# Small VectorE operations written as scalar-tensor-tensor with a constant column, in a four-layer graph attention kernel

## The chip, the core and the metric

The kernel runs on one core of a Trainium2 chip, as one launch. The metric is the device time of that core in microseconds (us). The kernel was run three times: 1598.85, 1600.91 and 1601.07 us, median 1600.91. One more execution was taken with the hardware profiler; it has a time of its own, 1596.83 us, and all durations below come from it.

The core's engines run side by side, each through its own list of instructions, and meet at semaphores: TensorE (PE, with its weight loads shown as PEld), VectorE (DVE), ScalarE (ACT), GpSimd (POOL) and SyncE (SP, which here only issues DMAs). The ordinary loads and stores are issued by SyncE, the indirect gathers by GpSimd.

## The reference

Four graph layers are applied one after the other to `x` (8 graphs, 2048 nodes, 64 features). All share one 2048 x 2048 adjacency matrix, which is sparse. Each layer is residual, with a normalisation ahead of it:

```python
h = jnp.maximum(_layernorm(x), 0.0);  x = x + _L0_gnn_ref(h, adj)
h = jnp.maximum(_layernorm(x), 0.0);  x = x + _L1_gnn_ref(h, adj, W1, a1)
h = jnp.maximum(_layernorm(x), 0.0);  x = x + _L2_gnn_ref(h, adj, Wh, bh, Wo, bo, gamma, beta)
h = jnp.maximum(_layernorm(x), 0.0);  x = x + _L3_gnn_ref(h, adj, W3, a3)
```

`_L0` is dot-product attention of a node over its neighbours: masked scores `h_n . h_m / 8`, softmax, weighted sum of `h_m`. `_L1` and `_L3` are additive attention: the score of an edge is `leaky_relu(f1_n + f2_m)`, where `f1` and `f2` are two projections of `h W`; what follows is elu or relu. `_L2` runs dot-product attention with four heads (the node itself counts as its neighbour), a leaky relu and an output projection, then a second dot-product attention on the result, then a layer norm with gamma and beta. A neighbour that is missing gets a large negative score, so it has no weight in the softmax.

## The kernel before

The kernel does not form the 2048 x 2048 scores. It turns the adjacency into lists of neighbours and works edge by edge. Nodes stand in 16 row tiles of 128 (`NT`), one node in each partition, with the features of all 8 graphs side by side (`F` = 512 columns, `B` = 8 graphs of `D` = 64). Nodes with low numbers have more neighbours, and a row tile `i` needs `ROWS[i]` slots (`K`) in which every node has one neighbour, and `PACKED[i]` slots (`T`) in which the further edges of the tile are packed 128 to a slot. `ROWS` holds 1 twice and 2 five times, `PACKED` holds 1 eight times; the total is 81 slots.

The work is done in five passes that read tables in HBM:

- First stage, up to about 350 us: `load_adj` and `lists` build the lists of a row tile from its rows of the adjacency, while the first attention layer runs on the tiles whose lists are ready. `lists` (L625 to L718) finds the neighbours with repeated maxima of eight on VectorE (L640, L652), lifts them off a constant (L645), turns them into gather indices (L662 for the row slots, L717 for the packed ones) and masks (L664, L680, L718), and makes the selection matrices that spread queries over packed edges (L689, L711). These arrays are narrow: L662 writes `K` numbers per partition, L664 writes `K - 1`, L717 and L718 write `T`. The sequence of L645, L654, L652, L657, L662 is a chain within VectorE. `lists` hands `idx` to the gathers, `mba` and `mbb` to the exponentials.
- Two additive layers (`additive(1, ...)` from about 350 to 600 us, and `additive(4, ...)` from about 1440 us to the end), whose scores are made at L540 to L549.
- The four-headed attention, about 600 to 1160 us (`score`, `weights`, `second2`).
- Its second attention, about 1160 to 1440 us (`first3` to `fourth3`), with L894 subtracting a row constant from the scores, and two normalisations for each tile.

A normalisation is `norm_a` (L257 to L276): sums of a row on VectorE (L261), then the mean (L265) and the centred rows (L268), either on GpSimd or on VectorE, as its caller asks; or, without centring, only the negative mean (L273). Its squares go to ScalarE, the rest is `norm_b`.

Neighbour rows are fetched by indirect DMAs that GpSimd issues (`gather`, L244), one for each slot, into a ring of 26 slots in SBUF. GpSimd also multiplies gathered rows with their weights in the first, third and fourth pass (`weigh_sum` L381 with GpSimd, `weights` L794 and L807), adds the residual (L480) and centres rows in the first stage. VectorE computes the products and sums of the scores (L423 to L432, L777, L781).

The order of the instructions on each engine is set by a scheduler: it takes the program as it is written tile by tile in `pipeline` (with lags between the stages of a tile) and orders each engine's list by an estimate of every instruction's duration. A changed instruction can therefore move its neighbours.

Behind the edge version stands a dense version (`gnn_stack`), which runs only if a check (`flag`) finds that the lists do not hold the adjacency. It isn't executed here.

Of the kernel before, what the change touches and what calls it, by code (L numbers as in the profile page):

```python
# [8 lines left out]
F32 = mybir.dt.float32  # L9
# [4 lines left out]
OP = mybir.AluOpType  # L14
AX = mybir.AxisListType

P = 128
NEG = -1.0e30
# [14 lines left out]
LIFT = 4096.0  # L33
# [32 lines left out]
def edge_stack(ctx: ExitStack, tc: tile.TileContext, x_in, adj, w1, w1t, a1, wh, wht, bh, wo, bo,  # L66
# [9 lines left out]
    nc = tc.nc  # L76
    N, F = x_in.shape
    D = gamma.shape[0]
    B = F // D
    NT = N // P  # L80
    H = bh.shape[0] // D
    INV_D = 1.0 / D
# [5 lines left out]
    const = ctx.enter_context(tc.tile_pool(name="const", bufs=1))  # L88
# [4 lines left out]
    nc.scalar.preload_act_table_set("natural_log_exp_and_others")  # L93
    eps = const.tile([P, 1], F32, name="eps")
    nc.gpsimd.memset(eps, EPS)
    ones = const.tile([P, 1], F32, name="ones")
    nc.gpsimd.memset(ones, 1.0 / N)

    idx = const.tile([P, NS], I32, name="idx")
    mba = const.tile([P, NS], F32, name="mba")  # L100
# [31 lines left out]
    def slots(t, i):  # L132
        return t[:, OFF[i]:OFF[i] + SLOTS[i]]
# [62 lines left out]
    def heads(t, n=B):  # L196
        return t.rearrange("p (b d) -> p b d", b=n)

    def wide(t, n=B):
        return t[:, :, None].to_broadcast([P, n, D])  # L200
# [22 lines left out]
    def rows(i, lo, hi, most=RING):  # L223

        t = lo
        while t < hi:
            at = (held[i] + t) % RING
            m = min(most, hi - t, RING - at)
            yield t, m, ring[:, at:at + m, :]
            t += m  # L230
# [24 lines left out]
    def rows_of(k, i):  # L255
        return table[k][i * P:(i + 1) * P, :F]

    def norm_a(src, st, centre, eng=nc.vector):

        s = small.tile([P, B], F32, name="ln_s")  # L260
        nc.vector.tensor_reduce(s, heads(src), AX.X, OP.add)  # L261
        st["sq"] = rows_pool[0].tile([P, F], F32, name="ln_sq", bufs=4)
        if centre:
            mean = small.tile([P, B], F32, name="ln_m")
            eng.tensor_scalar(mean, s, INV_D, None, op0=OP.mult)  # L265
            st["less"] = None
            st["src"] = rows_pool[0].tile([P, F], F32, name="ln_xc", bufs=3)
            eng.tensor_tensor(heads(st["src"]), heads(src), wide(mean), op=OP.subtract)  # L268
            nc.scalar.activation(st["sq"], st["src"], AF.Square)
            return  # L270
        st["src"] = src
        st["less"] = small.tile([P, B], F32, name="ln_m")
        nc.vector.tensor_scalar(st["less"], s, -INV_D, None, op0=OP.mult)  # L273
        for b in range(B):
            nc.scalar.activation(st["sq"][:, b * D:(b + 1) * D], src[:, b * D:(b + 1) * D], AF.Square,
                                 bias=st["less"][:, b:b + 1])  # L276
# [171 lines left out]
    def leaky(dst, src):  # L448
        return nc.vector.scalar_tensor_tensor(dst, src, SLOPE, src, op0=OP.mult, op1=OP.max)
# [21 lines left out]
    def divide(st, dst):  # L471
        nc.vector.tensor_tensor(heads(dst), heads(st["y"]), wide(st["rec"]), op=OP.mult)
# [40 lines left out]
    def additive(k, wd, *finish):  # L513
        def take(i, st):
            n = order.index(i)
            gather(k, i, st, taken[k, order[n - SPREAD]] if n >= SPREAD else None)

        def sums(i, st):
            w = slots(w_all, i)
            for t, m, g in rows(i, 0, SLOTS[i]):  # L520
                nc.scalar.activation(w[:, t:t + m], g[:, :, F:], AF.Exp, scale=1.0 / TEMP)
            d, p = by_query(i, w, B)
            S = seen[:, i, :]
            nc.vector.tensor_tensor(S, p, d, op=OP.add)

            z = small.tile([P, B], F32, name="z")
            nc.vector.tensor_scalar(z, S.bitcast(I32), TEMP * LN2 / 2 ** 23, -127.0 * TEMP * LN2, op0=OP.mult,
                                    op1=OP.add)
            nc.vector.tensor_tensor(z, z, f1s[:, i, 0, :], op=OP.add)
            leaky(f1s[:, i, 1, :], z)  # L530

        def first(i, st):
            K, T = ROWS[i], PACKED[i]
            w = slots(w_all, i)
            s = slots(s_all, i)
            n = 2 * B if k == 4 else B
            fs = f1s[:, i].rearrange("p t b -> p (t b)")[:, :n]
            pv = by_edge(i, fs, n)
            for t, m, g in rows(i, 0, K):
                nc.vector.tensor_tensor(s[:, t:t + m, :], g[:, :, F:], fs[:, None, :B].to_broadcast([P, m, B]),  # L540
                                        op=OP.add)
            for t, m, g in rows(i, K, K + T):
                nc.vector.tensor_tensor(s[:, t:t + m, :], g[:, :, F:], pv[:, t - K:t - K + m, :B], op=OP.add)
            taken[k, i] = leaky(s, s)
            if k == 4:
                nc.vector.tensor_tensor(s[:, :K, :], s[:, :K, :], fs[:, None, B:].to_broadcast([P, K, B]),
                                        op=OP.subtract)
                nc.vector.tensor_tensor(s[:, K:, :], s[:, K:, :], pv[:, :, B:], op=OP.subtract)
                nc.vector.tensor_scalar(s, s, 60.0, None, op0=OP.min)  # L549
            nc.scalar.activation(w, s, AF.Exp)  # L550
            wp = ps_w[0].tile([P, F], F32, name="w")[:, :(K + T) * B].rearrange("p (t b) -> p t b", b=B)
            nc.scalar.activation(wp, s, AF.Exp)
            st["wp"] = wp

        def check(i, st):
            second(i, st, st["wp"], seen[:, i, :] if k == 1 else None)

        def third(i, st):
            st["att"] = rows_pool[0].tile([P, F], F32, name="att")
            divide(st, st["att"])  # L560
            st["xt"] = transposed(st["att"])

        def project(i, st):
            p = st["p"] = ps_q.tile([P, F], F32, name="q")
            for j in range(F // P):
                nc.tensor.matmul(p[:, j * P:(j + 1) * P], st["xt"][:, j, :], wd, start=True, stop=True)
            finish[0](i, st)

        mid = [sums] if k == 4 else []
        pipeline(take, *mid, first, both(check, xs_rows), third, project, *finish[1:])  # L570

    def elu_add(i, st):
# [8 lines left out]
    with tc.tile_pool(name="rows", bufs=2) as rp:  # L581
        rows_pool[0] = rp
        sel_all[0] = rp.tile([P, sum(PACKED) * P], F32, name="sel", bufs=1)
        with tc.tile_pool(name="lists", bufs=2) as pool, \
# [39 lines left out]
            def lists(i, st):  # L624

                K, T, W = ROWS[i], PACKED[i], WIDTH[i]
# [15 lines left out]
                                nc.vector.match_replace(out=key[:, lo:hi], in_to_replace=c1[:, s, r, :],  # L642
                                                        in_values=key[:, lo:hi], imm_value=0.0)
                ends = c1.rearrange("p s r k -> p (s r k)")
                nc.vector.tensor_scalar(ends, ends, LIFT, 0.0, op0=OP.subtract, op1=OP.max)  # L645
                full = [s for s, (lo, hi) in enumerate(segs) if hi - lo > 8 * rounds]
                nc.vector.tensor_reduce(over[:, i, 0:1], c1[:, full[0]:, rounds - 1, 7:8].rearrange("p s o -> p (s o)"),
                                        AX.X, OP.max)
                ell = small.tile([P, W + 2], F32, name=f"ell{W}", bufs=2)
# [9 lines left out]
                at = OFF[i]  # L659
                me = nn[:, i:i + 1]  # L660
                nc.scalar.copy(ell[:, W + 1:W + 2], me)
                nc.vector.tensor_scalar(idx[:, at:at + K], ell[:, :K], -1.0, N + 1.0, op0=OP.mult, op1=OP.add)  # L662
                if K > 1:
                    nc.vector.tensor_scalar(mba[:, at + 1:at + K], ell[:, 1:K], 0.0, NEG, op0=OP.is_equal, op1=OP.mult)  # L664
                st8 = small.tile([P, 8], F32, name="st8")
                deg, half, nmid = st8[:, 0:1], st8[:, 1:2], st8[:, 2:3]
                junk = small.tile([P, W], F32, name=f"junk{W}", bufs=1)
# [9 lines left out]
                m = pm[:, P:P + K]  # L677
# [19 lines left out]
                ke = small.tile([P, max(PACKED)], F32, name="ke")[:, :T]  # L697
                V = W - K
                step = min(T, F // (V + 2))
                mp = mbb[:, at + K:at + K + T]  # L700
                for t0 in range(0, T, step):
# [7 lines left out]
                    for t in range(n):  # L709
                        eq = pool.tile([P, P], F32, name="eq")  # L710
                        nc.vector.scalar_tensor_tensor(eq[:, :V], iotaj[:, :V], col[:, t:t + 1], pv[:, t, :V],  # L711
                                                       op0=OP.is_equal, op1=OP.mult,
                                                       accum_out=ke[:, t0 + t:t0 + t + 1])
                    nc.vector.tensor_scalar(qidx[:, POFF[i] + t0:POFF[i] + t0 + n], pv[:, :, V + 1], -1.0, N + 1.0,
                                            op0=OP.mult, op1=OP.add)
                    nc.vector.tensor_tensor(mp[:, t0:t0 + n], ke[:, t0:t0 + n], pv[:, :, V + 1], op=OP.is_equal)
                nc.vector.tensor_scalar(idx[:, at + K:at + K + T], ke, -1.0, N + 1.0, op0=OP.mult, op1=OP.add)  # L717
                nc.vector.tensor_scalar(mp, mp, NEG, None, op0=OP.mult)  # L718

            pipeline(xin_rows, lambda i, st: norm_a(st["x"], st, True, nc.gpsimd), pre_b,  # L720
                     pre_c(None, nc.vector), pre_d(0, None))
# [152 lines left out]
    with tc.tile_pool(name="ps_q", bufs=3, space=bass.MemoryType.PSUM) as ps_q, \  # L874
# [11 lines left out]
        def first3(i, st):  # L886
            K = ROWS[i]
            sq = rows_pool[0].tile([P, F], F32, name="sq")
            nc.scalar.activation(sq, st["rows"], AF.Square)
            c = small.tile([P, B], F32, name="c3")  # L890
            nc.vector.tensor_reduce(c, heads(sq), AX.X, OP.add)
            s, w = scores(i, st, st["rows"]), slots(w_all, i)
            pv = by_edge(i, c, B)
            nc.vector.tensor_tensor(s[:, :K], s[:, :K], c[:, None, :].to_broadcast([P, K, B]), op=OP.subtract)  # L894
            nc.vector.tensor_tensor(s[:, K:], s[:, K:], pv, op=OP.subtract)
            exps(i, w, s, mbb, 1.0)

# [44 lines left out]
        v = small.tile([P, 4], F32, name="v", bufs=1)  # L942
# [520 lines left out]
```

## Time and profile before

| | |
|---|---|
| median of three runs | 1600.91 us |
| the profiled execution | 1596.83 us |
| its span, first to last instruction | 1595.0 us |
| mean granted TensorE clock | 0.899 |
| busy: PE, DVE, POOL, ACT | 1295.0, 1242.0, 1006.4, 768.0 us |
| gathers at L244 (405), GpSimd | 389.3 us, 961 ns each |
| GpSimd products L381, L794 | 156.6 us at 1736 ns; 307.2 us at 1918 ns |
| VectorE rows of the first stage, 120 to 270 us | 138.9 us busy of 150 |

"Busy" is the time in which an engine had an instruction running, and that includes the time in which a running instruction stands still inside the engine. A small VectorE instruction whose duration is far above that of its like is such a case: there is no idle time ahead of it that a semaphore explains, the time lies within it. This is why the mean of a group can hide two kinds of rows, and why groups are best read with different shapes kept apart.

A line of the groups holds: source line, engine, operation, output and inputs, their shapes, the count, then busy us and mean ns of one, then idle time before. A line of the timeline holds the start, the length, the engine, the source line and the operation.

### The profile page before, as it was taken

What the parts mean: (1) busy time and instruction counts of PE and PEld (TensorE: products, weight loads), DVE (VectorE), ACT (ScalarE), POOL (GpSimd) and SP (SyncE); (2) the same over time, 40 slices, a digit from 0 to 9 for tenths busy, and PEclk for the clock granted to TensorE, in tenths of its full rate; (3) what the DMA queues carried; (4) which work ended last, traced back from release to release, by engine and by line L of the source; (5) the groups of instructions that cost most, each with busy time, mean ns of one, the idle gap of its engine ahead of it and who ended that gap; (6) DMA issues with size and microseconds to landing.
All of it is one profiled execution on the core that took longest, in us unless ns stands there. A gap on an engine that the chain in (4) does not pass through costs nothing.

```text
span 1595.0 us, 16633 instructions
## 1 busy us (share of the span) xinstructions
PE 1295.0 (81%) x4280; PEld 671.0 (42%) x4280; DVE 1242.0 (78%) x2489; ACT 768.0 (48%) x2475; POOL 1006.4 (63%) x844
## 2 busy tenths in 40 slices
PE   3768898995989771899987999999747788975888
PEld 1624354564544430344343444443323354563555
DVE  5998989854689776999998799871159999974666
ACT  3424555672557781465541455555424446680111
POOL 6336777766750007998789889898278486306650
PEclk9997887987999996899999999999968798957899
DMA  7775654536874449465266345400085354136761
GB/s 216 233 244 158 201 183 152 198 107 182 260 253 153 173 164 348 161 232 173 88 209 204 111 141 182 158 14 7 27 321 154 93 179 126 67 103 204 244 205 69
DMA packets 88177, 266.99 MB, mean 167 GB/s; under 512 B 14957, under 2 KB 15001, under 8 KB 79881
## 3 DMA queue, kind: packets, MB, share of 16 engines
q0 software_dynamic: 37392, 141.05, 28.3%
q1 hardware_dynamic: 50680, 124.80, 22.6%
q8 instruction: 36, 0.59, 0.2%
q14 instruction: 69, 0.56, 0.1%
HBM read 208.74 MB, written 57.05 MB: 167 GB/s over the span
## 4 chain that ended last, share of the span: by engine, by line
PE 24%; DVE 13%; POOL 8%; DMA 7%; ACT 6%; issue 5%; SPq 0%; POOLq 0%; DVEq 0%; ACTq 0%
PE y L809 10%; DMA g<-table,idx 4%; POOL wh L794 3%; POOL g L244 3%; DMA rows<-table 3%; PE y L386 3%; PE y L801 2%; PE m L846 2%; ACT yn L817 2%; PE m L858 2%; DVE s L781 2%; DVE prod L777 2%; DVE prod L423 1%; POOL wh L807 1%; PE m L842 1%
## 5 line engine op out<-in xcount | busy, mean ns | idle before, releaser
L244 POOL DMA_INDIRECT g<-table,idx x405 | 389.3, 961 | 268.3 <-issue 115.6
L794 POOL TENSOR_TENSOR wh<-g,w 128x1024 f32<-128x1024 f32 x162 | 307.2, 1918 | 35.8 <-PE y L809 33.9
L386 PE MATMUL y<-wg,ident 128*128 128x512 f32 x392 | 223.0, 696 | 22.6 <-POOL wg L381 12.7
L381 POOL TENSOR_TENSOR wg<-g,w 128x1024 f32<-128x1024 f32 (+1 forms) x91 | 156.6, 1736 | 75.2 <-ACT w L437 65.9
L781 DVE TENSOR_REDUCE s<-prod 128x32 f32<-128x2048 f32 x81 | 183.9, 2286 | 20.2 <-ACT w L783 19.8
L809 PE MATMUL y<-wh,ident 128*128 128x512 f32 x320 | 155.6, 614 | 23.7 <-POOL wh L807 21.5
L386 PE MATMUL y<-wg,selt 128*128 128x512 f32 x256 | 135.1, 634 | 4.6 <-POOL wg L381 2.9
L809 PE MATMUL y<-wh,selt 128*128 128x512 f32 x256 | 123.1, 605 | 13.2 <-POOL wh L794 13.2
L817 ACT ACTIVATE yn<-y,rec 128x64 f32<-128x64 f32 x512 | 111.3, 367 | 29.7 <-PE y L809 29.0
L386 PEld LDWEIGHTS y<-wg,ident 128*128 128x128 f32 x392 | 79.0, 219 | 106.6 <-issue 66.2
L777 DVE TENSOR_TENSOR prod<-q,g 128x2048 f32<-128x2048 f32 x49 | 111.5, 2275 | 3.7 <-ACT g L775 3.3
L381 DVE TENSOR_TENSOR wg<-g,w 128x1024 f32<-128x1024 f32 (+1 forms) x92 | 98.9, 1086 | 11.3 <-PE y L386 9.5
L443 DVE SCALAR_TENSOR_TENSOR zt<-m,bhc,att 128x512 f32<-128x512 f32 x64 | 47.1, 737 | 75.3 <-ACT att L442 75.3
L809 PEld LDWEIGHTS y<-wh,ident 128*128 128x128 f32 x320 | 59.4, 195 | 98.6 <-issue 62.4
L400 PE MATMUL m<-w,selt 128*128 128x8 f32 (+1 forms) x384 | 58.8, 255 | 50.7 <-ACT w L437 16.5
L400 PEld LDWEIGHTS m<-w,selt 128*128 128x128 f32 x384 | 60.8, 205 | 92.9 <-ACT w L437 26.8
L775 ACT COPY g<-g 128x512 f32<-128x512 f32 x81 | 50.4, 622 | 84.5 <-DVE prod L777 83.6
L429 PE MATMUL q<-rows,sel 128*128 128x512 f32 x128 | 79.8, 725 | 12.7 <-DVE prod L431 4.7
L801 PE MATMUL y<-rows,ident 128*128 128x512 f32 x128 | 70.9, 640 | 19.6 <-DMA rows<-table 14.4
L777 DVE TENSOR_TENSOR prod<-qe,g 128x2048 f32<-128x2048 f32 x32 | 73.0, 2281 | 13.9 <-DMA qe<-qtab,qidx 12.7
L357 PE MATMUL m<-ones,xh 128*128 128x1 f32 x384 | 70.6, 307 | 10.7 <-DVE idx L717 3.5
L357 PEld LDWEIGHTS m<-ones,xh 128*128 128x128 f32 x384 | 70.8, 274 | 20.0 <-issue 13.2
(221 smaller groups left out, 2673.0 us busy)
## 6 DMA issues: line engine op xcount, KB each, us to landing
qtab<-q SPq DMA_DIRECT2D x16, 1040.0 KB, 4.1
a<-in_adj_dram SPq DMA_DIRECT2D x32, 512.0 KB, 5.1
q<-qtab SPq DMA_DIRECT2D x14, 1040.0 KB, 5.3
table<-xh SPq DMA_DIRECT2D x48, 256.0 KB, 3.3
rows<-table SPq DMA_DIRECT2D x48, 256.0 KB, 4.1
xs<-x SPq DMA_DIRECT2D x48, 256.0 KB, 2.2
x<-xs SPq DMA_DIRECT2D x48, 256.0 KB, 3.3
table<-xh SPq DMA_DIRECT2D x32, 260.0 KB, 2.1
```

The costliest lines, as they stand in the source:

```text
L244: g = nc.gpsimd.indirect_dma_start(out=ring[:, (held[i] + t) % RING, :cols], out_offset=None, in_=table[k][:, :], in_offset=bass.IndirectO ...
L357: nc.tensor.matmul(p[:, c:c + 1], xh[:, c * P:(c + 1) * P], ones, start=True, stop=True)
L381: eng.tensor_tensor(wg[:, :m].rearrange("p t (b d) -> p t b d", b=B), g[:, :, :F].rearrange("p t (b d) -> p t b d", b=B), w[:, t0:t0 + m, ...
L386: nc.tensor.matmul(y, lhs(i, t), wg[:, t - t0, :], start=(t == 0 and own is None), stop=(t == n - 1))
L400: nc.tensor.matmul(p[:, :cols], selt(i, t), packed[:, t, :], start=(t == 0), stop=(t == T - 1))
L429: nc.tensor.matmul(qe, sel(i, t - K), q, start=True, stop=True)
L777: nc.vector.tensor_tensor(pr.rearrange("p (b h) d -> p b h d", h=H), q[:, :B * H * D].rearrange("p (b h d) -> p b h d", h=H, d=D), heads(g ...
L781: nc.vector.tensor_reduce(s[:, t - lo, :], pr, AX.X, OP.add)
L794: nc.gpsimd.tensor_tensor(wg, heads(row(i, t))[:, :, None, :].to_broadcast([P, B, 2, D]), w[:, :, 2 * k:2 * k + 2, None].to_broadcast([P, ...
L801: nc.tensor.matmul(st["ys"][j], ident, xb[:, 4 * j:4 * j + 4], start=True, stop=False)
L809: nc.tensor.matmul(st["ys"][j], lhs(i, t), wg[:, 4 * j:4 * j + 4], start=False, stop=(t == n - 1))
L817: nc.scalar.activation(yn[:, b, h, :], st["ys"][j][:, b, h, :], AF.Copy, scale=st["rec"][:, 4 * j + b, 2 * k + h:2 * k + h + 1])
```

## The change

Three constant columns of 128 x 1 are made at the start: `zero` (0.0), `np1` (N + 1) and `neg1` (holds `NEG`). Small VectorE operations on SBUF data are then written as `scalar_tensor_tensor`, which computes `(in0 op0 scalar) op1 in1`, with one of these columns, repeated along the row, as `in1`. Where the operation already had two tensors, it keeps them and gets a factor of 1.0. Operations that GpSimd does, and those with an operand in PSUM, stay as they are. The numbers computed are the same.

```diff
+    zero, np1, neg1 = (const.tile([P, 1], F32, name=name) for name in ("zero", "np1", "neg1"))
+    for t, v in ((zero, 0.0), (np1, N + 1.0), (neg1, NEG)):
+        nc.gpsimd.memset(t, v)
...
+    def alike(t, like):
+        return t.to_broadcast(like.shape)
+
+    def times(dst, src, k):
+        nc.vector.scalar_tensor_tensor(dst, src, k, alike(zero, src), op0=OP.mult, op1=OP.add)
+
+    def less_from(dst, src):
+        nc.vector.scalar_tensor_tensor(dst, src, -1.0, alike(np1, src), op0=OP.mult, op1=OP.add)
...
-            eng.tensor_scalar(mean, s, INV_D, None, op0=OP.mult)
+            if eng is nc.vector:
+                times(mean, s, INV_D)
+            else:
+                eng.tensor_scalar(mean, s, INV_D, None, op0=OP.mult)
...
-            eng.tensor_tensor(heads(st["src"]), heads(src), wide(mean), op=OP.subtract)
+            if eng is nc.vector:
+                nc.vector.scalar_tensor_tensor(heads(st["src"]), heads(src), 1.0, wide(mean), op0=OP.mult,
+                                               op1=OP.subtract)
+            else:
+                eng.tensor_tensor(heads(st["src"]), heads(src), wide(mean), op=OP.subtract)
...
-        nc.vector.tensor_scalar(st["less"], s, -INV_D, None, op0=OP.mult)
+        times(st["less"], s, -INV_D)
...
-                nc.vector.tensor_tensor(s[:, t:t + m, :], g[:, :, F:], fs[:, None, :B].to_broadcast([P, m, B]),
-                                        op=OP.add)
+                nc.vector.scalar_tensor_tensor(s[:, t:t + m, :], g[:, :, F:], 1.0,
+                                               fs[:, None, :B].to_broadcast([P, m, B]), op0=OP.mult, op1=OP.add)
...
-                nc.vector.tensor_scalar(ends, ends, LIFT, 0.0, op0=OP.subtract, op1=OP.max)
+                nc.vector.scalar_tensor_tensor(ends, ends, LIFT, alike(zero, ends), op0=OP.subtract, op1=OP.max)
...
-                nc.vector.tensor_scalar(idx[:, at:at + K], ell[:, :K], -1.0, N + 1.0, op0=OP.mult, op1=OP.add)
+                less_from(idx[:, at:at + K], ell[:, :K])
                 if K > 1:
-                    nc.vector.tensor_scalar(mba[:, at + 1:at + K], ell[:, 1:K], 0.0, NEG, op0=OP.is_equal, op1=OP.mult)
+                    nc.vector.scalar_tensor_tensor(mba[:, at + 1:at + K], ell[:, 1:K], 0.0, alike(neg1, ell[:, 1:K]),
+                                                   op0=OP.is_equal, op1=OP.mult)
...
-                nc.vector.tensor_scalar(idx[:, at + K:at + K + T], ke, -1.0, N + 1.0, op0=OP.mult, op1=OP.add)
-                nc.vector.tensor_scalar(mp, mp, NEG, None, op0=OP.mult)
+                less_from(idx[:, at + K:at + K + T], ke)
+                times(mp, mp, NEG)
...
-            nc.vector.tensor_tensor(s[:, :K], s[:, :K], c[:, None, :].to_broadcast([P, K, B]), op=OP.subtract)
+            nc.vector.scalar_tensor_tensor(s[:, :K], s[:, :K], 1.0, c[:, None, :].to_broadcast([P, K, B]),
+                                           op0=OP.mult, op1=OP.subtract)
```

The subtraction at L546 (the fifth pass) is rewritten in the same way as L540. In the order of the list above these are the lines L265, L268, L273, L540, L645, L662, L664, L717, L718 and L894 of the kernel before.

More of the change, by code (lines that the diff above doesn't have):

```diff
@@ L545, in first @@
             if k == 4:
-                nc.vector.tensor_tensor(s[:, :K, :], s[:, :K, :], fs[:, None, B:].to_broadcast([P, K, B]),
-                                        op=OP.subtract)
+                nc.vector.scalar_tensor_tensor(s[:, :K, :], s[:, :K, :], 1.0,
+                                               fs[:, None, B:].to_broadcast([P, K, B]), op0=OP.mult,
+                                               op1=OP.subtract)
                 nc.vector.tensor_tensor(s[:, K:, :], s[:, K:, :], pv[:, :, B:], op=OP.subtract)
```

## The prediction

> **What bounds the kernel now.** I read the table of stretches first, to see which engine is full in the stages where the rewritten instructions stand. The columns are time, then busy microseconds and instruction count of PE, PEld, DVE, ACT and POOL, the granted clock, the DMA share and GB/s.
>
> ```profile
> 70.00:120.00 50.00, 31.22 (x84) 13.08 (x83) 47.24 (x259) 14.12 (x26) 17.16 (x18) 1.00 0.66 215
> 120.00:170.00 50.00, 37.85 (x111) 19.03 (x111) 44.79 (x187) 23.97 (x71) 32.77 (x31) 0.75 0.60 186
> 170.00:220.00 50.00, 45.35 (x148) 20.88 (x148) 49.83 (x148) 26.36 (x85) 42.27 (x36) 0.94 0.58 188
> 220.00:270.00 50.00, 43.45 (x159) 24.75 (x159) 44.24 (x142) 25.73 (x100) 39.56 (x35) 0.77 0.48 148
> 270.00:320.00 50.00, 46.84 (x182) 29.30 (x182) 40.41 (x104) 32.21 (x129) 37.24 (x34) 0.86 0.55 190
> 360.00:600.00 240.00, 193.65 (x682) 103.91 (x682) 179.68 (x318) 150.73 (x446) 83.55 (x101) 0.92 0.60 200
> 1160.00:1440.00 280.00, 215.45 (x707) 120.70 (x707) 241.53 (x460) 152.61 (x529) 156.10 (x124) 0.79 0.44 144
> ```
>
> VectorE is the fullest engine of the first stage: 138.9 of the 150 us from 120 to 270, and 47.2 of the 50 before that. In the fourth pass (1160 to 1440) it has 241.5 of 280. The chain of waits reaches back only to about 590 us, so for the first stage the table has to serve. Next, the groups of instructions kept apart by shape (busy us, mean ns of one | idle before):
>
> ```profile
> L645 DVE TENSOR_SCALAR c<-c 128x64 f32<-128x64 f32 x14 | 8.4, 602 | 0.0
> L664 DVE TENSOR_SCALAR mba<-ell 128x2 f32<-128x2 f32 x6 | 7.4, 1236 | 0.0
> L664 DVE TENSOR_SCALAR mba<-ell 128x3 f32<-128x3 f32 x1 | 3.7, 3745 | 0.0
> L664 DVE TENSOR_SCALAR mba<-ell 128x1 f32<-128x1 f32 x5 | 0.7, 141 | 0.0
> L718 DVE TENSOR_SCALAR mbb<-mbb 128x3 f32<-128x3 f32 x2 | 3.3, 1635 | 0.0
> L718 DVE TENSOR_SCALAR mbb<-mbb 128x1 f32<-128x1 f32 x8 | 1.1, 142 | 0.0
> L894 DVE TENSOR_TENSOR s<-s,c 128x24 f32<-128x24 f32 x6 | 3.6, 602 | 0.0
> ```
>
> Two or three numbers per partition cannot take 1.2 to 3.7 us of arithmetic, while one number takes 0.14. The timeline shows what the long ones do (start us, us):
>
> ```profile
> 177.15 3.76 POOL L381 TENSOR_TENSOR wg<-g,w 128x1024 f32<-128x1024 f32 x2
> 178.14 2.81 DVE L664 TENSOR_SCALAR mba<-ell 128x2 f32<-128x2 f32 x1
> ...
> 193.47 1.92 POOL L381 TENSOR_TENSOR wg<-g,w 128x1024 f32<-128x1024 f32 x1
> 193.48 0.14 DVE L664 TENSOR_SCALAR mba<-ell 128x1 f32<-128x1 f32 x1
> ...
> 42.85 1.04 POOL L268 TENSOR_TENSOR ln_xc<-x,ln_m 128x512 f32<-128x512 f32 x1
> 43.45 0.99 DVE L313 SCALAR_TENSOR_TENSOR xh<-ln_xc,ln_r 128x512 f32<-128x512 f32 x1
> ...
> 1274.85 3.77 POOL L381 TENSOR_TENSOR wg<-g,w 128x1024 f32<-128x1024 f32 x2
> 1276.06 2.61 DVE L894 TENSOR_TENSOR s<-s,c 128x24 f32<-128x24 f32 x1
> ```
>
> At 178.14 a two-element tensor_scalar stands until both GpSimd products are over (180.91). At 193.48 a one-element one runs straight through a GpSimd product. The third pair matters most: a scalar_tensor_tensor with both inputs in SBUF, 0.68 us at its other places, takes 0.99 because GpSimd's subtraction runs until 43.89. The fourth is a tensor_tensor of two SBUF inputs that waits through two products. So three kinds of VectorE instruction wait for GpSimd: tensor_scalar of more than one element, tensor_tensor from SBUF and SBUF, and scalar_tensor_tensor from SBUF and SBUF.
>
> [...]
>
> **The change part by part.**
>
> 1. *tensor_scalar of two or more elements becomes scalar_tensor_tensor with a constant column* (L645 all 16; L662 14; L664 9; L717 8; L718 8; the 48 means at L265 and L273). [...] By the third pair it still waits for GpSimd. [...] no trace row here has a second input that never moves, so this is bounded from both sides. Upper end 0. Lower end, all waits gone: 14 x (0.602-0.18) = 5.9 at L645; 6.5 + 3.6 at L664; 2.1 + 0.4 at L662; 1.3 + 0.7 at L717; 3.0 + 0.4 at L718; together 24 us of VectorE in the first stage. I take 0, since L313's second input is itself one value repeated 64 times.
>
> 2. *tensor_scalar of one element becomes two-input.* By the shapes there are 23: 2 at L662, 5 at L664, 8 at L717, 8 at L718. They have no wait today (0.134 to 0.145 us) and get one. Two ways to size it. (a) The 55 longer rows of those five lines lose 24 us, 0.43 each; 23 x 0.43 = 10 us. (b) Laid on today's timeline, the one-element rows that start under a GpSimd tensor instruction, or in the last 0.4 us of a gather's descriptor work, stand at 193.48 (1.9 us to go), 252.12 and 253.27 (0.5 and 0.4), and 294.99 (4.7 us of GpSimd instructions end to end; the L718 behind it waits in the same gap): 7.5 us. Not all is on the path: after 294.99 VectorE has about 3.2 us of idle gaps (0.5 + 0.3 + 0.8 + 1.7) that take up part of the 4.7. So 1.9 + 0.9 + 1.5 = 4.3 us. What queues behind is the list building itself: L652's next maximum, then the indices that the gathers of this row tile need. Bounds: 0, if everything is absorbed, and 10.
>
> 3. [...] 14 rows of 128x64 go from about 0.18 to 0.204 (L449 at that size): 0.35 us. The 128x352 row goes from 0.329 to about 0.35 + 0.15 = 0.50, and the 128x128 row gains under 0.1. Sum 0.6 us, on VectorE in the full stage.
>
> 4. *tensor_tensor becomes scalar_tensor_tensor with a factor 1* (L540, L546, L894, and VectorE's L268). Two SBUF inputs before and after: 160 to 200 ns for the short ones, 680 for 512 elements either way (L313). The waits at L268 and L894 in the fourth pass (2.2 and 4.0 us in all) and at L265 (1.6) stay. Cost 0; lower end, under the same doubt as in part 1, 7.8 us of VectorE, of which perhaps a quarter is on the path, since there the chain runs mostly over loads of rows and matmuls.
>
> 5. *Three GpSimd memsets at the start.* Neighbours of this shape take 0.10 us and start 0.03 apart: 0.1 us. GpSimd stands idle 1.59 us from 10.16 on behind a DMA, but that DMA is issued later too, so up to 0.1 us stays. Counted as 0.1.
>
> 6. *Order.* The scheduler moves instructions. With both programs' lists side by side, VectorE's rows shift by at most 29 places, GpSimd's by at most 6 (70 of about 1,000 rows), SyncE's by at most 4 (69 of 396; loads and stores of x, rows and table swapped with their neighbours). The first 1,000 VectorE rows hold the large shifts; in the fourth pass there are many small ones, elsewhere few. No dependency is new but the three columns. I take 0 and keep a spread: the first stage's 24 us are some eight long waits of 2 to 3.7 us and a tail of short ones. With eleven expected over 78 exposed rows the count varies by about 3, so 3 x 2.6 us x 0.6 on the path = 5 us either way.
>
> Sum: 0 + 4.3 + 0.6 + 0 + 0.1 = 5 us more than the profiled execution's 1596.83 (span 1595.0), so 1601.8. The median of the runs shown is 4.1 above that execution, so against 1600.91 the forecast is 1606.
>
> **The rivals.**
> [...] The 24 us of VectorE waits in the first stage go, and the new ones do not come. With 0.7 of them on the path (VectorE is 90% busy there) that is 17, and 2 from the fourth pass: 1582, faster. It decides once more than a fifth of those waits vanish (5 of 24). [...] Against: L313, and L268, whose second input repeats a value too and waits at 1317.16 for 2.0 us.
> *The new waits hide.* GpSimd's and TensorE's own work (POOL 42 of 50, PE 45 of 50 from 170 to 220) is next in line, and the stage ends when it did: about 1601.
> *Placement decides.* The long waits fall elsewhere; the same mechanism gives 1612 with three more of them, 1595 with fewer.
>
> **How the numbers follow.** My case 0.55; free column 0.12; hidden 0.12; placement worse 0.11, better 0.10. About 0.2% (3.2 us) is what a measurement of this kernel can tell from no change. My case, with its own spread of 5 us, gives slower 0.43, same 0.09, faster 0.03; hidden gives same 0.09, slower 0.02, faster 0.01; the others fall on one side. Slower 0.56, same 0.18, faster 0.26. The range 1589 to 1614 leaves out the free column and a very bad placement. Slower alone: 1604.5 to 1614.
>
> **What would show it.** One-element rows at L662, L664, L717 and L718 over 0.3 us under a GpSimd product prove part 2; at 0.15 throughout they refute it. Rewritten rows of two or more elements with multi-microsecond durations that end with a GpSimd tensor instruction prove part 1; if all are below 0.25 us, the free column is right. VectorE's busy time from 27 to 300 should grow by some 8 us, passes two, three and five should keep theirs. A fourth pass that is faster by several us, or an end of the first stage that moves with neither, would make the forecast wrong.

## The result, and the profile after

The changed kernel takes 1622.39 us (median of 4 runs, 1619.8 to 1625.94), against 1599.88 us for the kernel before on the same chip (4 runs). The ratio is 1.0142, with a 95% interval of 1.012 to 1.0164: the change costs about 22.5 us, more than four times what was forecast. The profiled execution took 1619.8 us, with a span of 1617.6.

The first question is where in the program the time went. Stage ends can be read from the timeline. The first stage ends with its last residual add on GpSimd, the first additive layer with the last VectorE row that prepares the queries of the next pass (L333 before), the four-headed attention with its last VectorE row, and the fourth pass with the last addition of beta.

| stage (us) | before | after | longer by |
|---|---|---|---|
| first stage | 349.4 | 361.4 | 12.0 |
| first additive layer | 258.2 | 255.3 | -2.9 |
| four-headed attention | 541.4 | 542.6 | 1.2 |
| fourth pass | 275.5 | 288.8 | 13.3 |
| last layer, to the end of the span | 170.4 | 169.6 | -0.8 |

Two stages carry the loss. The 13.3 us of the fourth pass come from one profile of each kernel, and they are not exact: in `e_relu`, `e_idx` and `e_mp` below, VectorE's list of that pass is the one of before, and it took 277.5 to 282.7 us where the profile before has 275.5. The table of stretches of the changed kernel answers to the one of before, with the same columns (time, then busy us and count of PE, PEld, DVE, ACT, POOL, then clock, DMA share, GB/s):

```profile
120.00:170.00 50.00, 38.39 (x112) 19.06 (x113) 42.98 (x193) 24.75 (x72) 32.42 (x31) 0.77 0.56 181
170.00:220.00 50.00, 43.67 (x131) 19.31 (x132) 47.41 (x137) 21.93 (x73) 36.58 (x31) 0.89 0.50 164
220.00:270.00 50.00, 42.96 (x156) 23.04 (x155) 39.41 (x132) 25.07 (x97) 36.91 (x33) 0.80 0.48 151
270.00:320.00 50.00, 40.15 (x161) 25.37 (x159) 41.29 (x108) 29.29 (x116) 40.14 (x35) 0.80 0.58 194
1160.00:1440.00 280.00, 206.45 (x653) 111.85 (x652) 247.00 (x448) 143.38 (x488) 158.22 (x127) 0.80 0.44 145
```

From 120 to 270 VectorE was busy for 138.9 us before; now it is 129.8. So in the first stage VectorE does not stand inside more of its instructions, it stands idle in front of them. In the fourth pass it is the other way round: 241.5 us busy became 247.0, with fewer rows done in that time (448 after 460).

**First stage.** The view of waits says whom VectorE waits for (us in total, times, longest). Before, from 75 us to the stage's end:

```profile
DVE prod L431 <- PE q L429: 5.6, 5, 1.8
...
DVE col L708 <- PE m L706: 2.9, 5, 0.9
...
DVE st L673 <- PE m L671: 2.0, 2, 1.6
```

After, in the same stretch:

```profile
DVE col L729 <- PE m L727: 11.0, 6, 4.1
DVE st L694 <- PE m L692: 5.0, 3, 3.2
...
DVE prod L450 <- PE q L448: 3.2, 5, 0.9
```

The rows that take the packed edges' columns (`col`) and counts (`st`) out of PSUM now wait 16.0 us for TensorE, after 4.9 us. All lines of the view add up to 29.0 us before and 39.6 after. That accounts for the growth of VectorE's idle time in this stretch, from 33.5 to 43.8. The timeline of the changed kernel shows the longest one, with what TensorE did before it (start, length, engine, row; the bracket is the wait ahead of it):

```profile
225.36 0.34 DVE L710 TENSOR_SCALAR sel<-q,st 128x128 f32<-128x128 f32 x1
...
225.98 2.07 PE L405 MATMUL y<-wg,ident 128*128 128x512 f32 x2 [1.62 <-POOL wg L400]
...
227.84 1.71 PE L405 MATMUL y<-wg,selt 128*128 128x512 f32 x2
...
229.50 0.29 PE L727 MATMUL m<-ell,sel 128*128 128x15 f32 x2
...
229.83 0.16 DVE L729 TENSOR_TENSOR col<-pe,m 128x1 f32<-128x1 f32 x1 [4.05 <-PE m L727]
229.90 0.22 DVE L672 MAX8 ell<-c 128x8 f32<-128x64 f32 x1
230.04 0.67 DVE L273 TENSOR_REDUCE ln_s<-x 128x8 f32<-128x512 f32 x1
```

For 4.05 us VectorE stands at the `col` row. The two rows listed behind it, a maximum over list ends and a row sum, do not read `col`, and they start 0.07 and 0.21 us after it. TensorE's own list has a part in it: the selection matrix `sel` that its matmul reads is written by 225.70, but TensorE does the weighted sums (L405) first, and the first of those had waited 1.62 us for GpSimd's product.

**The waits for GpSimd.** The groups of the changed kernel, shapes apart (busy us, mean ns of one | idle before):

```profile
L284 DVE SCALAR_TENSOR_TENSOR ln_xc<-z,ln_m 128x512 f32<-128x512 f32 x16 | 18.4, 1149 | 0.1
L284 DVE SCALAR_TENSOR_TENSOR ln_xc<-x,ln_m 128x512 f32<-128x512 f32 x16 | 12.4, 774 | 0.1
...
L684 DVE SCALAR_TENSOR_TENSOR mba<-ell,neg 128x3 f32<-128x3 f32 x1 | 6.6, 6611 | 0.0
L684 DVE SCALAR_TENSOR_TENSOR mba<-ell,neg 128x2 f32<-128x2 f32 x6 | 6.5, 1077 | 0.0
L915 DVE SCALAR_TENSOR_TENSOR s<-s,c 128x24 f32<-128x24 f32 x6 | 4.7, 787 | 0.0
L665 DVE SCALAR_TENSOR_TENSOR c<-c,zero 128x64 f32<-128x64 f32 x14 | 3.9, 279 | 0.0
L268 DVE SCALAR_TENSOR_TENSOR idx<-ke,np 128x1 int32<-128x1 f32 x8 | 3.8, 474 | 0.0
L265 DVE SCALAR_TENSOR_TENSOR mbb<-mbb,zero 128x1 f32<-128x1 f32 x8 | 3.4, 428 | 0.0
...
L665 DVE SCALAR_TENSOR_TENSOR c<-c,zero 128x352 f32<-128x352 f32 x1 | 0.5, 508 | 0.0
```

The one-element rows have gone from 145 and 142 ns to 474 and 428: they wait now. Rows of two and three elements wait as they did. Yet the sum over all rewritten list rows of what each takes above 0.17 us, which I call list waits below, is 23.2 us after 23.9: the new waits came, and others went away (the 14 rows of 128x64 fell from 602 to 279 ns).

The centring of `z` in the fourth pass is the other change: 1149 ns a row, after 733. One of its rows in the timeline of the changed kernel:

```profile
1209.98 0.95 POOL L247 DMA_INDIRECT g<-table,idx  x1 [0.30 <-DVE ln_m L265]
1210.56 3.85 DVE L284 SCALAR_TENSOR_TENSOR ln_xc<-z,ln_m 128x512 f32<-128x512 f32 x1
...
1210.94 2.91 POOL L400 TENSOR_TENSOR wg<-g,w 128x1024 f32<-128x1024 f32 x2
```

It starts just ahead of two GpSimd products, takes 3.85 us in place of 0.68, and ends 0.56 us after them. Over the fourth pass the centring rows take 9.0 us above 0.68 each, their median before (2.2 before), the rows of L894/L915 6.7 us above 0.17, again the median before (3.9 before) and the means 3.8 above 0.16 (1.7 before). That is 11.7 us more, against a growth of 11.3 in VectorE's busy time there (238.0 to 249.3).

The theory from this: the loss is neither the form of the rows nor their waits as such, but the other order in which the scheduler lists the same work. The rival: the new waits of the rewritten rows, which all have names in the traces, cost the time themselves.

### The profile page after: what moved, and what is told of

Its sections match the earlier page's. It is cut to its first block, busy times and chain, and to the rows that moved or that the text cites. A ratio compares the mean times of both kernels' runs of the same rounds, so it can differ in the third digit from the quotient of the medians.

```text
span 1617.6 us, 16632 instructions
## 1 busy us (share of the span) xinstructions
PE 1300.2 (80%) x4280; PEld 670.7 (41%) x4280; DVE 1253.6 (77%) x2489; ACT 768.3 (47%) x2475; POOL 1007.3 (62%) x847
## 5 line engine op out<-in xcount | busy, mean ns | idle before, releaser
L405 PE MATMUL y<-wg,ident 128*128 128x512 f32 x392 | 223.5, 695 | 25.2 <-POOL wg L400 16.9
L405 PE MATMUL y<-wg,selt 128*128 128x512 f32 x256 | 140.3, 654 | 3.1 <-DVE wg L400 1.6
L830 PE MATMUL y<-wh,selt 128*128 128x512 f32 x256 | 127.0, 622 | 10.6 <-POOL wh L815 10.6
L405 PEld LDWEIGHTS y<-wg,ident 128*128 128x128 f32 x392 | 78.1, 217 | 108.2 <-issue 64.5
L346 PE MATMUL q<-q,xt 128*128 128x512 f32 x128 | 67.0, 639 | 17.4 <-DVE prod L348 9.1
```

What stands on the lines that cost most here:

```text
L405: nc.tensor.matmul(y, lhs(i, t), wg[:, t - t0, :], start=(t == 0 and own is None), stop=(t == n - 1))
L830: nc.tensor.matmul(st["ys"][j], lhs(i, t), wg[:, 4 * j:4 * j + 4], start=False, stop=(t == n - 1))
```

## The experiments

Each ratio is to runs of the kernel before on the same chip. The chips differ: the kernel before took 1643.69 us on that of the first four, 1641.52 on that of the next four, 1600.15 on that of the last four.

**Form and order apart.** Four kernels. `e_order` lets the scheduler order the changed program and turns the rows with a constant column back into the two-constant form afterwards, each in its place. `e_form` does the reverse: the program of before is scheduled, then the rows are turned into the new form in place. `e_memsets` has only the three columns, `e_pairs` only the rewriting of two-tensor rows with a factor of 1.0.

`e_order`, to the changed kernel:

```diff
         whole_stack(tc, t, out)
+    turn_back(nc)
...
+        if name in value:
+            imm = mybir.ImmediateValue(dtype=F32, value=value[name])
+            return mybir.InstTensorScalarPtr(op0=i.op0, op1=i.op1, ins=[i.ins[0], i.ins[1], imm], **same(i))
```

`e_form`, to the kernel before (`how` holds the rows of the lines L265, L273, L645, L662, L664, L717 and L718):

```diff
         whole_stack(tc, t, out)
+    turn(nc)
...
+        if i.name not in how:
+            return None
...
+        return mybir.InstTensorScalarPtr(op0=i.op0, op1=op1, is_scalar_tensor_tensor=True,
+                                         ins=[i.ins[0], i.ins[1], col], **same(i))
```

> The changed kernel with its order of instructions held exactly, every operation with a constant column turned back into the tensor_scalar it was (the four rewritten two-tensor operations stay scalar_tensor_tensor). Order theory (the scheduler's new order puts the waiting rows under GpSimd products): most of the 22 us stays, 1614 or more. Form theory (one-element rows wait anew, the others wait longer): back to 1600 to 1606, and the one-element rows of the list building are at 0.15 us again.

> The kernel before with three memsets and the order that the scheduler gives it so; after scheduling, the tensor_scalar rows are turned into the constant-column form in place. Form theory: 1610 to 1622, one-element rows of the list building with means of 0.4 us or more. Order theory: no more than 5 us above the run with the memsets alone.

> The kernel before with the three constant columns and their memsets, and nothing that uses them. Both theories: 1600 within 3 us. If it is off by more, a few instructions that the scheduler moves for no reason of duration already cost that, and order alone is a strong lever.

> The kernel before with only the four two-tensor operations (centring on VectorE, scores of the additive layers, row constant) written as scalar_tensor_tensor; its order is that of the kernel before on every engine. Order theory: 1600 within 2 us. Rival, that scalar_tensor_tensor waits for GpSimd where tensor_tensor does not: the fourth pass is some 10 us longer, 1608 to 1614, and the centring of z is near 1.1 us instead of 0.73.

Measured: `e_order` 1.017 (1.0136 to 1.0204), `e_form` 1.0006 (0.9986 to 1.0026), `e_memsets` 1.0003 (0.9986 to 1.002), `e_pairs` 1.0001 (0.9985 to 1.0017). The new order with the constant-column rows in their old form has the whole loss; the new form in the old order has none that can be told. The groups of `e_form` show that its rows do wait:

```profile
L674 DVE SCALAR_TENSOR_TENSOR mba<-ell,neg 128x2 f32<-128x2 f32 x6 | 8.5, 1417 | 0.0
...
L674 DVE SCALAR_TENSOR_TENSOR mba<-ell,neg 128x1 f32<-128x1 f32 x5 | 3.1, 613 | 0.0
L728 DVE SCALAR_TENSOR_TENSOR idx<-ke,np 128x1 int32<-128x1 f32 x8 | 1.8, 220 | 0.0
```

List waits are 28.5 us in `e_form` and 21.4 in `e_memsets`, so 7.1 us more. But VectorE's idle time from 75 us to the end of the first stage is 33.3 us instead of 37.9, so that stage ends only 2.5 us later (354.7 and 352.2), and nothing of it can be told at the end. By these two profiles, most of the new waits fill time in which VectorE would have stood idle.

**Which line brings the order.** `e_645` has the three columns and only L645 in the new form, `e_means` only L265 and L273, `e_but645` is the changed kernel with only L645 as it was before.

```diff
-                nc.vector.tensor_scalar(ends, ends, LIFT, 0.0, op0=OP.subtract, op1=OP.max)
+                nc.vector.scalar_tensor_tensor(ends, ends, LIFT, alike(zero, ends), op0=OP.subtract, op1=OP.max)
...
-            eng.tensor_scalar(mean, s, INV_D, None, op0=OP.mult)
+            if eng is nc.vector:
+                times(mean, s, INV_D)
+            else:
+                eng.tensor_scalar(mean, s, INV_D, None, op0=OP.mult)
```

The first pair of lines is `e_645` (and, reversed, `e_but645`), the rest with the like of it at L273 is `e_means`.

> The kernel before with the memsets and L645 alone in the constant-column form. Its first stage stands in the order of the changed kernel, the fourth pass in that of the kernel before. Theory: the first stage's order costs 6 to 10 us by itself, the wait of VectorE for TensorE at the packed-edge columns (L706 to L708) is near 11 us from 120 to 310 as in the changed kernel (2.9 before), the fourth pass is unchanged: ratio 1.004 to 1.007. Rival, that the loss needs the rewritten instructions themselves: 1.000.

> The kernel before with the memsets and only the means (L265, L273) in the constant-column form; mostly the fourth pass changes its order. Theory: the fourth pass becomes 8 to 13 us longer through centring and row constants that wait inside for GpSimd (9 and 7 us in the changed kernel, 2 and 4 before), the first stage stays: ratio 1.005 to 1.008. Rival, that the fourth pass suffers only from what the first stage hands on: 1.000 to 1.002.

> The changed kernel with L645 alone turned back before scheduling, so the scheduler makes a third order for the first stage and keeps that of the fourth pass. If L645's estimated duration is what spoils the first stage: 1.005 to 1.009, with the fourth pass still long. If any new order of the first stage costs as much: 1.012 or more. If orders differ by luck, anything from 1.000 to 1.015.

Measured: `e_645` 1.0127 (1.008 to 1.0174), about twice what was expected of it; `e_means` 1.0034 (1.0015 to 1.0052), less than expected; `e_but645` 1.0145 (1.0113 to 1.0177). One line of 15 rows reproduces nearly the whole loss, and taking that same line out of the change does not bring it back. The lines do not have prices that add up. Each set of edits gives another order, and the orders differ.

Three expectations rested on orders or waits that the traces do not show. `e_645` was taken to leave the fourth pass in the order of before; but in the traces 148 of VectorE's 453 rows in it have to change places to turn one list into the other (155 in the changed kernel), and the pass took 293.1 us. `e_but645` was taken to keep the fourth pass of the changed kernel, and has a third order there. In `e_means` the centring was to stand 9 us for GpSimd and the row constants 7, in a fourth pass that is 8 to 13 us longer; they stood 2.9 and 3.6 us, and the pass took 284.5 us, within the 281.8 to 286.4 of the kernels without loss (`e_form`, `e_pairs`, `e_memsets`).

**One line's order without its form.** The last doubt is whether the 15 rows of L645 cost something themselves. `e_645_order` takes the order of `e_645` and turns these rows back after scheduling, so that, but for the three columns, every instruction is one of the kernel before.

```diff
         whole_stack(tc, t, out)
+    turn_back(nc)
```

> The order that the scheduler makes when only the line of the list ends (`ends`, 15 rows) is written with the constant column, but with those 15 rows turned back into the two-constant form after scheduling, so that every instruction is the one of the kernel before. Theory (the scheduler's order is the whole loss, and the form costs nothing): the ratio to before stays near 1.0127, the value of the kernel with only that line in the new form, at 1.009 to 1.016; the first stage is some 3 to 5 us and the fourth pass some 6 to 10 us longer than in the kernel that only has the three columns. Rival (the 15 waiting rows themselves cost half of it or more): 1.000 to 1.006.

Measured: 1.0105 (1.0081 to 1.013), inside the theory's band and outside the rival's. On every engine the rows stand in the order that they have in `e_645`. The first stage ends at 355.5 us and the fourth pass takes 288.1. In its waits from 75 us to the first stage's end, and in its groups, the two signs are there again, with no rewritten row in the program:

```profile
DVE col L720 <- PE m L718: 10.3, 6, 3.3
...
DVE st L685 <- PE m L683: 4.5, 2, 3.1
```

```profile
L280 DVE TENSOR_TENSOR ln_xc<-z,ln_m 128x512 f32<-128x512 f32 x16 | 17.5, 1096 | 0.5 <-ACT xh L304 0.4
...
L906 DVE TENSOR_TENSOR s<-s,c 128x24 f32<-128x24 f32 x6 | 4.7, 790 | 0.0
```

The centring takes 1096 ns as the two-tensor row that it always was. So the collision with GpSimd's products comes with the order, which sets when a row runs, and not with the row's form.

**Rows that leave VectorE.** If waits inside VectorE can be had back, small rows should go to an engine that shows no such wait. In the profile before, ScalarE's rows of 128x8 at L282 have a median of 0.30 us both inside a GpSimd `TENSOR_TENSOR` (19 rows, 0.36 at most) and clear of one (51 rows). `e_scalar` moves L645, L662, L717 and L718 to ScalarE; `e_relu` only L645, `e_idx` only L662 and L717, `e_mp` only L718. The lines of the three smaller ones together are `e_scalar`:

```diff
+    np1, low = (const.tile([P, 1], F32, name=name) for name in ("np1", "low"))
+    for t, v in ((np1, N + 1.0), (low, -LIFT)):
+        nc.gpsimd.memset(t, v)
...
+                nc.scalar.activation(ends, ends, AF.Relu, bias=low)
...
+                nc.scalar.activation(idx[:, at:at + K], ell[:, :K], AF.Identity, scale=-1.0, bias=np1)
...
+                nc.scalar.activation(idx[:, at + K:at + K + T], ke, AF.Identity, scale=-1.0, bias=np1)
+                nc.scalar.activation(mp, mp, AF.Copy, scale=NEG)
```

> The kernel before with L645, L662, L717 and L718 done by ScalarE (L664 stays on VectorE), so that nothing but L664 of the list building can wait for GpSimd. If the 24 us that VectorE stands in such waits in the first stage bound it: 5 to 12 us faster, 0.992 to 0.997. If they are hidden, as the run with the forms turned in place suggests (7 us more of them, no change): 1.000, or worse by the order.

> The kernel before with the list ends (15 rows) moved to ScalarE as a Relu with a bias column. The order on VectorE then differs from before only in the first stage; from the second layer to the fourth pass the VectorE rows stand as before. Theory (half of the loss comes from the fourth pass's order): the fourth pass keeps 275 to 285 us on a chip where before takes 1640 (its length within 3 us of before's), and the ratio is 0.996 to 1.004, set by the first stage alone. Rival (any change to the ends' line lengthens the fourth pass, by the time at which it is entered): fourth pass 8 us or more longer, ratio 1.007 or more.

> The kernel before with the index rows of both lists (15 and 8 rows) moved to ScalarE as Identity with scale -1 and a bias column. VectorE's order differs from before in the first stage and in single places after it, not in the fourth pass. Theory (the order of the fourth pass decides half): fourth pass within 3 us of before's; VectorE waits for GpSimd in the first stage 3 to 6 us less than the 21 to 24 us of before; ratio 0.994 to 1.003. Rival (waits removed in the first stage are paid back by rows that come later): ratio 1.003 to 1.008.

> The kernel before with the middle mask's scaling (8 one-element rows) moved to ScalarE. These rows do not wait in the kernel before (some 0.14 us each), so the form is worth 1 us at most; the order on VectorE moves some 340 rows, all in the first stage and the last pass. Theory (only order and what VectorE waits for in it count): ratio 0.997 to 1.005, with the first stage's length following the wait of the packed-edge column rows for TensorE. Rival (moving rows at all costs): 1.005 to 1.012.

Measured: `e_scalar` 1.0029 (1.001 to 1.0048), `e_relu` 0.9977 (0.9961 to 0.9994), `e_idx` 0.9977 (0.9961 to 0.9992), `e_mp` 0.9989 (0.9976 to 1.0003). In `e_scalar` the list waits on VectorE fall to 2.2 us, and the first stage ends at 342.8 us, 9.4 sooner than in `e_memsets` on a chip about as fast. If all of that comes from the 19 us of waits that went, about half of them was on the path. But the order of its fourth pass came out different too, that pass takes 295.9 us, and the gain is gone. `e_relu` and `e_idx` were chosen because VectorE's order in the fourth pass stayed as before. Both are faster than the kernel before by 0.23%, about 3.7 us, and than the changed kernel by 26 us or so. The centring shows it in `e_relu`, and its Relu rows show what they cost on ScalarE:

```profile
L271 DVE TENSOR_TENSOR ln_xc<-z,ln_m 128x512 f32<-128x512 f32 x16 | 11.7, 732 | 0.0
...
L648 ACT ACTIVATE c<-c,low 128x64 f32<-128x64 f32 x14 | 4.8, 344 | 2.0 <-DVE st L675 1.7 <-DVE c L643 0.2
```

Three expectations missed in detail. In `e_mp` the first stage was to follow the wait of the packed-edge columns for TensorE: the `col` and `st` rows waited 11.4 us there, after 4.9, and the stage ended at 348.3 us, 1.1 sooner than before. The list waits of `e_idx` fell to 5.8 us, far more than the 3 to 6 us by which they were to fall, since the remaining rows were listed elsewhere. And the fourth passes took 280.6 us (`e_relu`) and 282.7 (`e_idx`), 5 and 7 us above the 275.5 of the profile before, where 3 was the bound; neither the rival's 8 us nor its total came.

The runs side by side, in profiled us:

| kernel | ratio | first stage ends | fourth pass | list waits | centring and L894, above work |
|---|---|---|---|---|---|
| before | 1 | 349.4 | 275.5 | 23.9 | 6.1 |
| after | 1.0142 | 361.4 | 288.8 | 23.2 | 15.7 |
| `e_645_order` | 1.0105 | 355.5 | 288.1 | 20.3 | 14.7 |
| `e_relu` | 0.9977 | 348.3 | 280.6 | 15.1 | 5.9 |
| `e_idx` | 0.9977 | 344.2 | 282.7 | 5.8 | 6.9 |
| `e_mp` | 0.9989 | 348.3 | 277.5 | 18.3 | 9.5 |
| slower chips: `e_memsets` | 1.0003 | 352.2 | 286.4 | 21.4 | 5.7 |
| `e_form` | 1.0006 | 354.7 | 281.8 | 28.5 | 6.0 |
| `e_pairs` | 1.0001 | 353.0 | 282.5 | 24.2 | 6.3 |
| `e_order` | 1.017 | 359.3 | 293.3 | 21.9 | 14.7 |
| `e_645` | 1.0127 | 356.6 | 293.1 | 21.7 | 15.0 |
| `e_means` | 1.0034 | 353.2 | 284.5 | 24.7 | 6.6 |
| `e_but645` | 1.0145 | 364.0 | 291.6 | 15.5 | 14.0 |
| `e_scalar` | 1.0029 | 342.8 | 295.9 | 2.2 | 10.6 |

The list waits do not go with the ratio: `e_form` has the most and no loss, `e_but645` few and a large loss. The last column does, over 13 in every kernel that lost a per cent or more and under 11 in all others.

What stays open: that the `col` and `st` waits make up the first stage's share is read from the traces of the changed kernel and of `e_645_order`, in which they match the growth of idle time. They are no sure sign of a loss: in `e_idx` they are 14.4 us and the stage ends at 344.2 us, with 18 us less of list waits. No kernel was made that moves these rows alone, and since the new orders differ on TensorE and ScalarE too, which engine's list does the harm is not shown. In the first stage, the new orders without the constant-column rows lost 6.1 us (`e_645_order`, after the profile before) and 7.1 (`e_order`, after `e_memsets`), where the changed kernel lost 12.0; with one profile of each, a part for the new waits in that stage is not excluded. Nor do the runs show why the scheduler's choice is so much worse in these orders.

## Why the prediction was wrong

The direction was right. The time, 1606, was 16 us too low and the result is above the range. By its own steps:

- *Part 1 (rows of two or more elements still wait, 0):* right. `mba<-ell,neg` of 128x3 stood for 6.6 us; the free column, the rival in which the waits go, is refuted.
- *Part 2 (one-element rows begin to wait, 4.3 us on the path):* the mechanism is right, the size is not. The 7.1 us of added list waits in `e_form` are near the 7.5 of the timeline method, but by luck: 3.1 us of them stand at the 23 one-element rows (5.0 in the changed kernel), the other 4.0 at the 55 longer ones, whose change part 1 had put at 0. What reached the end looks smaller than 4.3: `e_form` stands 0.0003 above `e_memsets`, 0.5 us; but each ratio is only known to about 3 us, so 4.3 is not excluded. Most of the waits took the place of idle time. I had looked for such cover behind one row (3.2 us after 294.99) and not over the whole stage, where VectorE was idle for 33.5 us from 75 us on.
- *Part 3 (the wide rows at L645, 0.6 us):* right in size; the 128x352 row took 508 ns, forecast 500. That forecast was an estimate; a straight line through 204 ns for 64 elements (L449) and 680 ns for 512 (L313) gives 510.
- *Parts 4 and 5 (0 and 0.1):* right as to the form. `e_pairs` and `e_memsets` are at 1.0001 and 1.0003, and in `e_pairs` the centring of `z` took 737 ns after 733. But part 4 also said that the waits at L268, L894 and L265 stay, and in the new order they did not: that belongs to part 6.
- *Part 6 (order: "I take 0 and keep a spread", 5 us either way):* this is the step that failed. The order alone cost 1.05% (`e_645_order`) to 1.7% (`e_order`), 17 to 27 us. Two things were wrong in it. The spread was made from one mechanism, the count of long waits for GpSimd in the first stage; that total did not move at all (23.9 to 23.2), while in the changed kernel VectorE's waits for TensorE at `col` and `st`, 4.9 us before and not in the sum, grew to 16.0. And the "many small" shifts in the fourth pass were seen and given nothing, although VectorE had 241.5 of 280 us there and the rows at L268 and L894 were known to wait for GpSimd: moved by a few places they cost 9.6 us more.

The rival "placement decides" (1612) named the right cause with half the size and the wrong carrier; its two figures, 1612 and 1595, are also not the 5 us either way of part 6, which give 1611 and 1601. The sign for which I asked, VectorE's busy time from 27 to 300 us growing by some 8 us, did not show: it fell from 249.5 to 243.6. From 75 us to the end of the first stage it grew by 1.7 us, and its idle time by 10.3. The end of the first stage moved by 12.0 us without that growth, which is the sign that the prediction had named for its being wrong.

## What to carry to other kernels

Where a scheduler orders by estimated durations, rewriting an instruction is also a reordering, and the reordering can cost more than anything that is counted per instruction; here ten sets of small edits gave ratios from 0.998 to 1.015. Turning the form back after scheduling, or on in the old order, separates the two with one kernel each. Before a wait is charged to the end of a stage, set it against that engine's idle time over the whole stage; and price a moved row by every engine that its neighbours can wait for, in each pass in which rows move.

## What the runs showed of the hardware

In the changed kernel's timeline a row of three elements starts while a gather's `DMA_INDIRECT` runs on GpSimd, and then stands through four tensor instructions, each of which starts within 0.06 us of the end of the one before:

```profile
273.01 0.95 POOL L247 DMA_INDIRECT g<-table,idx  x1 [0.31 <-PE q L319]
...
273.37 6.61 DVE L684 SCALAR_TENSOR_TENSOR mba<-ell,neg 128x3 f32<-128x3 f32 x1
273.99 1.91 POOL L400 TENSOR_TENSOR wg<-g,w 128x1024 f32<-128x1024 f32 x1
275.84 1.04 POOL L287 TENSOR_TENSOR ln_xc<-x,ln_m 128x512 f32<-128x512 f32 x1
276.84 1.26 POOL L499 TENSOR_TENSOR x<-x,att 128x512 f32<-128x512 f32 x1
278.06 1.89 POOL L400 TENSOR_TENSOR wg<-g,w 128x1024 f32<-128x1024 f32 x1
```

It ends at 279.98, 0.03 us after the last of them. Not every row stood to the end of such a sequence: a one-element row at 304.64 us (L268) took 0.67 us and ended at 305.31, while the two GpSimd products around it ran from 303.40 to 307.16, the second from 305.26 on. The runs show how long these rows stood, and not what in the hardware holds them.

The gather alone did not hold such rows in the changed kernel: sixteen rewritten list rows of one to four elements start while a gather runs, and each took 0.16 us or less. For fourteen of them the gather was followed 0.3 us later by another, for two (at 262.87 and 263.05) by a tensor instruction at once. Two more rows with a tensor instruction within 0.01 us behind the gather, at 177.38 and 197.86, stood through it, for 4.12 and 2.13 us. In the kernel before, a two-element row at 141.13 us took 0.37 us where 0.40 of a gather was left, and another at 205.15 took 0.16 where 0.46 was left.

And chips differ by more than the effect studied: the same kernel before took 1600.15 us on one chip and 1643.69 on another, 2.7% more, so only ratios within one chip say anything here.
